# A macaron block of mixture-of-experts, attention and a gated scan: second expert weights kept in SBUF, row tables cleared first, and part of the tails' normalisation moved to ACT

## The chip, the core and the metric

The kernel runs on one core of one Trainium2 chip. The metric is the device time of one execution in microseconds. A core has TensorE (PE, matrix products; its weight loads are listed apart as PEld), VectorE (DVE), ScalarE (ACT), GpSimd (POOL) and SyncE (SP, which here issues nearly all plain DMAs). POOL issues the indirect DMAs, which scatter or gather rows by an index. All data are 32-bit floats; a matrix product of such data runs as two passes, so a count of matmuls in the profile is twice that of the program.

## The reference

The input `x` is 8 sequences of 512 tokens with 128 features. Six residual steps follow each other, each on a layer norm (LN) of `x`:

```
x = x + 0.5 * moe(LN(x))       # 8 experts, 128 -> 512 -> 128, ReLU, each token goes to its best 2
x = x + attention(LN(x))       # 16 heads of 8, rotary positions, causal softmax
x = x + 0.5 * moe(LN(x))       # the same weights
x = x + 0.5 * fp6_linear(LN(x))
x = x + mix(LN(x))
x = x + 0.5 * fp6_linear(LN(x))

moe:        logits = x @ router_w + router_b;  two best, gates = softmax of the two
            y_e = relu(x @ W1[e] + b1[e]) @ W2[e] + b2[e];  out = sum of gate * y_e
fp6_linear: x and weight are rounded, in blocks of 32, to a 6-bit float grid times
            max|block| / 7.5; then x @ weight.T + bias
mix:        n = rmsnorm(x) * w; g, v, d = three linear maps of n
            h_t = a_t * h_(t-1) + sigmoid(g) * tanh(v), a = 0.001 + 0.998 * sigmoid(d)
            u = x + h; m = rmsnorm(u) * w2; out = u + (silu(m @ W_gate) * (m @ W_up)) @ W_out
```

## The kernel before

`X[b]`, the 512 tokens of sequence `b`, stays in SBUF as four tiles of 128 tokens by 128 features. Everything else is written as operations of a graph (`add`): each has one or more engines that it may run on with estimated costs, the buffers that it reads, writes and acquires, and dependencies. `Graph.search` is a list planner. It walks through the graph with a clock of its own, gives each operation an engine and a place, each buffer a slot of its kind, and repeats this 12 times with adapted priorities. The order that it finds best is issued as it is, engine by engine, and semaphores keep the data right; so a change of one cost or one dependency moves many instructions.

Stage 0 is the first expert layer (`moe_front`, `moe_tiles`, `moe_combine` with s = 0), then `attention`, then stage 2, the second expert layer, then a `tail` for each sequence (`fp6` with s = 3, `mix`, `fp6` with s = 5, store). The planner lets stages of different sequences overlap.

The expert layer. Sequences are taken in groups: 2, 3 and 3 of them in stage 0, four groups of 2 in stage 2. `moe_front` normalises, computes logits, picks two experts for each token, and gives each token two places in a table of rows in DRAM in which an expert's rows lie together, padded to tiles of 128. POOL scatters the rows (L783), one indirect DMA for 128 rows. DVE also writes `eids`, the expert of each tile. There are 23 tiles for a group of two and 31 for one of three, 177 in all. `moe_tiles` takes tiles in pairs. For each tile SP reads the expert's number into a register and loads that expert's whole weights into `wx` (L813, L814):

```
r = nc.sync.value_load(state["eids"].t[0:1, i : i + 1], min_val=0, max_val=NE - 1)
nc.sync.dma_start(out=wxi.t, in_=wexp[bass.ds(r, 1), :, :]...)
```

`wx` is 128 x 1156: W1, W2, b2 and b1; six of them exist. SP loads the rows `xs` (L824), PE turns them (`xp`, L835), ACT or DVE copies them to `xt`, PE multiplies by W1 (`hp`, L846), ACT applies bias and ReLU (`hs`, L858), PE multiplies by W2 (`yp`, L867), DVE adds b2 (`yo`, L876), SP stores to a second table (L881). When all tiles of the group are stored, `moe_combine` gathers each token's two rows (POOL, L898) and adds them with their gates (DVE, L911). The table `rows_in` has to be zero where no row is scattered: each of the four tables is cleared by a DMA from a 128 x 128 tile of zeros (L467), the first one behind the loads of `x`, the others later ("late" loads, with the constants of attention and tails).

Attention works in bursts: `sa` (scores for the maxima, L1018), DVE takes row maxima of them (L1070), `sb` (scores again, transposed), ACT's exponential (L1081), POOL cuts the diagonal blocks (L1089), and `av` (L1125). Expert tiles of stage 0 and of stage 2 run between bursts.

The tails. `normed` takes statistics on DVE: four `bn_stats` (L558), four `bn_aggr` (L564), a small sum (L570, or L566 to L568 for a root mean of squares), then POOL raises to the power -1/2 (L581). `scaled_rows` scales the four tiles, on ACT (L598, L600, after L592 on DVE) or on DVE (L602, L604), as the planner chooses. `quantized` finds each block's largest value (L1207), scale and inverse and the negated scale (L1202 to L1204), multiplies by the inverse (L1211, POOL or DVE), finds from the exponent bits how coarse the grid is there (`iz`, and its inverse `iv`, L1224), multiplies (L1226), rounds with a large constant (L1228), corrects ties (L1231, L1233), multiplies by `iv` (L1235, DVE) and then by the negated scale (L1238, POOL or DVE). PE turns the result and multiplies it by the quantized weight (L1271).

Of the kernel before, what the change touches and what calls it, by code (L numbers as in the profile page):

```python
# [39 lines left out]
E_W1, E_W2, E_B2, E_B1 = 0, NFC * P, 2 * NFC * P, 2 * NFC * P + P  # L40
E_ALL = E_B1 + NFC

# [15 lines left out]
TURNED = (0,)  # L58

# [43 lines left out]
class Op:  # L103

    __slots__ = "alts fn acq bufs deps succ left prio start end eng ready bulk order skew idx pace occ".split()
# [26 lines left out]
class Graph:  # L132
# [4 lines left out]
    def add(self, alts, fn, r=(), w=(), acq=(), deps=(), order=(), bulk=0, skew=0.0, pace=0.0):  # L137
# [3 lines left out]
        o.succ, o.start, o.end, o.eng, o.idx = [], None, None, None, len(self.ops)  # L141
        needs = {id(d): d for d in deps}
# [26 lines left out]
    def levels(self):  # L169
        for o in reversed(self.ops):  # L170
            e, t, lat, _ = o.alts[0]
            if e == "PE":
                lat = t + 0.3
            if o.bulk:
                lat = 2.2 + o.bulk / 330e3
            o.prio = max(
                [s.prio + (lat if o in s.deps else 0.0) for s in o.succ], default=lat
            ) + o.skew

# [19 lines left out]
    def refine(self, order, span, first):  # L199
# [13 lines left out]
        for o, f in zip(self.ops, first):  # L213
            o.prio = MIX * (span - late[id(o)]) + (1 - MIX) * o.prio
# [132 lines left out]
def kernel(  # L347
# [3 lines left out]
    wexp: bass.AP,  # L351
    rw: bass.AP,
# [53 lines left out]
    late = []  # L406
# [7 lines left out]
    def load_late(b, ap, bulk):  # L414
        late.append(lambda after: add(
# [6 lines left out]
    def const(name, ap, is_late=False):  # L422
# [4 lines left out]
        return (load_late if is_late else load)(b, ap, n)  # L427
# [23 lines left out]
    zero = filled("zero", [P, P], 0.0)  # L451
# [3 lines left out]
    n_0 = len(GROUPS[0])  # L455
    rows_in, rows_out = [], []
    for g in range(n_g):
        n = max(tiles_of(len(gs[g])) for gs in GROUPS.values() if g < len(gs)) * TW
# [3 lines left out]
    def clear_rows(g, order, skew=0.0):  # L462
        t = rows_in[g].t
        n = t.shape[0]
        return add(
            dma(0),
            lambda e: nc.sync.dma_start(  # L467
                out=t.rearrange("(n p) c -> p n c", p=P),
                in_=zero.t.unsqueeze(1).to_broadcast([P, n // P, P]),
            ),  # L470
            r=[zero], w=[rows_in[g]], bulk=n * P * 4, order=order, skew=skew,
        )

    for b in range(2, nb):
        load_x(b)
    sp.append(clear_rows(0, sp[-1:], 1e4))
    for g in range(1, n_g):
        late.append(lambda after, g=g: clear_rows(g, [groups[0, min(g, n_0) - 1]["sent"][-1]]))
    rope_s = const("rope_s", rope, True)
    wattn_s = const("wattn_s", wattn, True)  # L480
    future_s = const("future_s", future, True)
    vec_s = const("vec_s", vecs, True)
    wq8_s = const("wq8_s", wq8, True)
    wmix_s = const("wmix_s", wmix, True)
    wout_s = const("wout_s", wout, True)
    half_bq = fixed("half_bq", [P, P])
    load_late(half_bq, bq.partition_broadcast(P), P * P * 4)
# [6 lines left out]
    def clear_for_attention(after):  # L494
# [4 lines left out]
        for v in vpad:  # L499
# [5 lines left out]
            for k in range(2):  # L505
# [3 lines left out]
                    w=[v], order=[after])  # L509

# [41 lines left out]
    def normed(src, view, name, eps, skew=0.0, squares=False):  # L552
# [7 lines left out]
        def go(e):  # L560
# [4 lines left out]
            if squares:  # L565
                nc.vector.tensor_tensor(sm.t[:, 36:40], mv[:, :, 0], mv[:, :, 0], ALU.mult)  # L566
                nc.vector.tensor_tensor(sm.t[:, 32:36], sm.t[:, 36:40], mv[:, :, 1], ALU.add)
                nc.vector.tensor_scalar_add(sm.t[:, 32:36], sm.t[:, 32:36], eps)  # L568
            else:
                nc.vector.tensor_scalar_add(sm.t[:, 32:36], mv[:, :, 1], eps)  # L570
# [4 lines left out]
        add(("DVE", 0.4 + 0.2 * squares, 0.5 + 0.2 * squares, None), go, w=[sm], skew=skew)  # L575
# [53 lines left out]
    def moe_front(s, g):  # L629
# [5 lines left out]
        GT, NTL = n_b * NT, tiles_of(n_b)  # L635
# [141 lines left out]
        for n in range(n_b):  # L777
            for k in range(2):
                for t in range(NT):
                    i = n * NT + t  # L780

                    def scatter(e, n=n, k=k, t=t, i=i):
                        ins = nc.gpsimd.indirect_dma_start(  # L783
                            out=rows_in[g].t[0 : NTL * TW, :],
# [7 lines left out]
                        ("POOL", 1.02, 2.2, None), scatter, r=[us[n], (keep, f"at{k}"), (rows_in[g], ("s", name, i, k))],  # L792
# [3 lines left out]
    def moe_tiles(s, g):  # L796

        NTL = tiles_of(len(GROUPS[s][g]))
        state = groups[s, g]
        for j in range((NTL + 1) // 2):  # L800
            tiles = [i for i in (2 * j, 2 * j + 1) if i < NTL]
# [7 lines left out]
            for i in tiles:  # L809
                wx[i] = buf("wx", "wx", f"wx_{name}")  # L810

                def fetch(e, i=i, wxi=wx[i]):
                    r = nc.sync.value_load(state["eids"].t[0:1, i : i + 1], min_val=0, max_val=NE - 1)  # L813
                    nc.sync.dma_start(  # L814
                        out=wxi.t, in_=wexp[bass.ds(r, 1), :, :].rearrange("o p c -> p (o c)")
# [3 lines left out]
                    ("SP", 0.73, 3.0, None), fetch, r=[state["eids"]], w=[wx[i]], acq=[wx[i]],  # L819
# [3 lines left out]
            def rows_of(e, xs=xs, rows=rows, halves=halves):  # L823
                ins = nc.sync.dma_start(  # L824
                    out=halves(xs.t), in_=rows_in[g].t[rows, :].rearrange("(h p) c -> p h c", p=P)
# [4 lines left out]
                dma(0), rows_of, w=[xs], acq=[xs], deps=state["sent"], bulk=w * P * P * 4, order=rows_loads[-1:]  # L830
# [32 lines left out]
            for h, i in enumerate(tiles):  # L863

                def second(e, h=h, i=i, yp=yp, hs=hs, wx=wx):
                    for fc in range(NFC):
                        nc.tensor.matmul(  # L867
                            yp.t[:, ts(h, P)], hs[i].t[:, ts(fc, P)],
                            wx[i].t[:, E_W2 + fc * P : E_W2 + (fc + 1) * P],
# [3 lines left out]
                add(pe(P, NFC), second, r=[hs[i], wx[i]], w=[(yp, h)], acq=[yp, yo] if h == 0 else [])  # L873
# [6 lines left out]
            def store(e, yo=yo, rows=rows, halves=halves):  # L880
                state["stored"].append(nc.sync.dma_start(  # L881
                    out=rows_out[g].t[rows, :].rearrange("(h p) c -> p h c", p=P), in_=halves(yo.t)
# [477 lines left out]
    for g in range(n_0):  # L1360
        moe_front(0, g)
        if g + 1 < n_0:
            late.pop(0)(None)
# [100 lines left out]
```

## Time and profile before

| what | value |
|---|---|
| runs | 1100.86, 1101.2, 1102.36 us (median 1101.2) |
| the profiled execution | 1096.83 us, its span 1095.1 us |
| mean granted TensorE clock | 0.932 |
| busy | PE 929.3, PEld 694.7, DVE 752.4, ACT 515.3, POOL 536.1 us |
| bytes moved by DMA | 163.60 MB |
| of these, weight loads `wx` | 177 of 578 KB each |
| scatters and gathers | 128 and 128 |

The span runs from the first to the last instruction. A page slices it into 40 equal parts and prints for each the busy share in tenths. "issue" in a list of waits is time in which the engine waited for nothing that the profile shows. A queue name such as SPq is the engine's sequencer, which handles registers, semaphores and DMA issues.

### The profile page before, as it was taken

To read this page: it belongs to the slowest core of one execution; us is meant where nothing else is said; L and a number is where in the kernel's file an instruction comes from. 1 tells how busy PE (TensorE), PEld (TensorE's weight loads), DVE (VectorE), ACT (ScalarE), POOL (GpSimd) and SP (SyncE) were. 2 spreads that over 40 slices of the span, in tenths; PEclk is the share of its full clock that TensorE was granted. 3 is DMA by queue.
4 is the path that set the end of the run, shared out by engine and by line. 5 is a ranking of instruction groups with operands and counts; after the bars stand their busy time and mean duration, and the time that the engine had idled before them with its cause. 6 is when DMAs were issued, how large, how long until landed. Compare 5 with 4: busy or idle time off the path is not lost.

```text
span 1095.1 us, 22590 instructions
## 1 busy us (share of the span) xinstructions
PE 929.3 (85%) x7282; PEld 694.7 (63%) x7282; DVE 752.4 (69%) x2797; ACT 515.3 (47%) x1335; POOL 536.1 (49%) x681
## 2 busy tenths in 40 slices
PE   5357958799899989998999999998978989976873
PEld 5357946677667764554765776666877878535452
DVE  7501216278866579997786667966338859999996
ACT  3123523235465654555755665564435536543521
POOL 2771053525722168447246223784048654774552
PEclk9978968799999998999998999999989989988985
DMA  4737969487455411015233354233978876100001
GB/s 147 261 113 250 384 196 331 132 297 225 132 191 158 145 56 50 26 36 182 64 117 100 107 155 141 76 122 93 303 266 270 264 245 214 30 17 1 20 19 39
DMA packets 102070, 163.60 MB, mean 149 GB/s; under 512 B 11200, under 2 KB 70720, under 8 KB 101952
## 3 DMA queue, kind: packets, MB, share of 16 engines
q1 hardware_dynamic: 93760, 145.37, 41.1%
q0 software_dynamic: 8192, 16.79, 5.1%
q8 instruction: 58, 0.95, 0.3%
q14 instruction: 60, 0.49, 0.1%
HBM read 129.28 MB, written 29.16 MB: 145 GB/s over the span
## 4 chain that ended last, share of the span: by engine, by line
PE 50%; DVE 21%; issue 10%; POOL 8%; DMA 6%; another core or an unknown queue 2%; ACT 1%; SPq 1%; POOLq 0%; DVEq 0%; ACTq 0%
PE hp L846 11%; PE yp L867 10%; PE sb L1018 8%; PE sa L1018 7%; PE av L1125 5%; DMA wx<-in_wexp 3%; DVE sa L1070 3%; POOL y L898 3%; POOL rows_in L783 1%; PE xp L835 1%; PE lp L663 1%; DMA y<-rows_out,keep 1%; DVE q L1226 1%; DVE x L911 1%
## 5 line engine op out<-in xcount | busy, mean ns | idle before, releaser
L858 ACT ACTIVATE hs<-hp,wx 128x128 f32<-128x128 f32 x704 | 199.5, 372 | 231.0 <-PE hp L846 115.4
L1070 DVE CUSTOM_DVE_ANT_0 sa<-sa,future_s 128x384 f32<-128x384 f32 (+3 forms) x512 | 241.1, 514 | 86.6 <-PE sa L1018 50.8
L867 PE MATMUL yp<-wx,hs 128*128 128x128 f32 x1416 | 199.1, 287 | 56.3 <-issue 30.2
L1081 ACT ACTIVATE pm<-sb 128x512 f32<-128x512 f32 x320 | 173.3, 598 | 147.5 <-PE sb L1018 67.3
L867 PEld LDWEIGHTS yp<-wx,hs 128*128 128x128 f32 x1416 | 180.7, 200 | 67.8 <-issue 53.6
L846 PE MATMUL hp<-xt,wx 128*128 128x128 f32 x1416 | 200.5, 289 | 9.2 <-DMA wx<-in_wexp 5.1
L1018 PE MATMUL sb<-qa,ka 32*128 32x256 f32 (+3 forms) x1024 | 198.0, 467 | 10.3 <-DVE nstat L1070 6.8
L846 PEld LDWEIGHTS hp<-xt,wx 128*128 128x128 f32 x1416 | 183.1, 202 | 31.4 <-issue 11.8
L1089 POOL TENSOR_SCALAR_AFFINE_SELECT pm<-pm 128x256 f32<-128x256 f32 x256 | 104.3, 426 | 199.2 <-ACT pm L1081 196.6
L1018 PE MATMUL sa<-ka,qm 32*128 32x384 f32 (+3 forms) x1024 | 191.9, 474 | 4.2 <-DVE qm L537 2.4
L898 POOL DMA_INDIRECT y<-rows_out,keep x128 | 136.2, 1064 | 89.7 <-PE yp L867 47.9
L783 POOL DMA_INDIRECT rows_in<-um,keep x128 | 128.7, 1005 | 70.4 <-DVE route L751 32.9
L876 DVE TENSOR_TENSOR yo<-yp,wx 128x128 f32<-128x128 f32 x177 | 48.7, 285 | 124.1 <-PE yp L867 65.3
L1018 PEld LDWEIGHTS sb<-qa,ka 32*128 32x128 f32 x1024 | 98.3, 186 | 49.2 <-DVE nstat L1070 16.7
L1018 PEld LDWEIGHTS sa<-ka,qm 32*128 32x128 f32 x1024 | 88.3, 189 | 31.7 <-issue 7.9
L1125 PE MATMUL av<-pm,vpad 128*32 128x256 f32 (+3 forms) x1024 | 80.4, 445 | 1.8 <-POOL pm L1089 1.3
L535 DVE COPY xt<-xp 128x256 f32<-128x256 f32 (+1 forms) x83 | 33.8, 408 | 59.2 <-PE xp L835 27.4
L1070 DVE DVE_READ_ACCUMULATOR2_ANT nstat<- 128x1 f32 x512 | 72.0, 141 | 0.0
L1125 PEld LDWEIGHTS av<-pm,vpad 128*32 128x32 f32 x1024 | 28.7, 111 | 59.2 <-issue 41.1
L911 DVE SCALAR_TENSOR_TENSOR x<-y,keep,x 128x128 f32<-128x128 f32 x128 | 45.3, 368 | 20.6 <-DMA y<-rows_out,keep 18.6
L835 PE MATMUL xp<-cst,xs 128*128 128x128 f32 x177 | 36.3, 287 | 12.5 <-DMA xs<-rows_in 12.0
L835 PEld LDWEIGHTS xp<-cst,xs 128*128 128x128 f32 x177 | 22.6, 148 | 17.3 <-issue 14.6
(215 smaller groups left out, 1233.6 us busy)
## 6 DMA issues: line engine op xcount, KB each, us to landing
wx<-in_wexp SPq DMA_DIRECT2D x177, 578.0 KB
xs<-rows_in SPq DMA_DIRECT2D x85, 128.0 KB
rows_out<-yo SPq DMA_DIRECT2D x85, 128.0 KB
rows_in<-zero SPq DMA_DIRECT2D x2, 1984.0 KB
rows_in<-zero SPq DMA_DIRECT2D x2, 1472.0 KB
x<-in_x SPq DMA_DIRECT2D x8, 256.0 KB
rows_in<-um,keep POOLq DMA_INDIRECT x128
y<-rows_out,keep POOLq DMA_INDIRECT x128
```

The source lines that it names most:

```text
L783: ins = nc.gpsimd.indirect_dma_start(out=rows_in[g].t[0 : NTL * TW, :], out_offset=bass.IndirectOffsetOnAxis(ap=at(k)[:, i : i + 1], axis= ...
L835: nc.tensor.transpose(xp.t[:, ts(h, P)], halves(xs.t)[:, h, :], ident)
L846: nc.tensor.matmul(hp.t[:, ts(fc, P)], wx[i].t[:, E_W1 + fc * P : E_W1 + (fc + 1) * P], xt.t[:, ts(h, P)], start=True, stop=True,)
L858: nc.scalar.activation(o, a, AF.Relu, bias=bias)
L867: nc.tensor.matmul(yp.t[:, ts(h, P)], hs[i].t[:, ts(fc, P)], wx[i].t[:, E_W2 + fc * P : E_W2 + (fc + 1) * P], start=(fc == 0), stop=(fc == ...
L898: ins = nc.gpsimd.indirect_dma_start(out=tokens(y)[:, t, :], out_offset=None, in_=rows_out[g].t[0 : NTL * TW, :], in_offset=bass.IndirectO ...
L911: nc.vector.scalar_tensor_tensor(X[b].t[:, t, :], tokens(y)[:, t, :], state["gates"](k)[:, i : i + 1], X[b].t[:, t, :], ALU.mult, ALU.add,)
L1018: nc.tensor.matmul(sc.t[:, at : at + hi - lo], stat.t[rows, ts(m, P)], mov.t[rows, lo:hi], start=True, stop=True,)
L1070: nc.vector.tensor_tensor_reduce(out=sc.t[:, at : at + wd], in0=sc.t[:, at : at + wd], in1=future_s.t[:, S - wd : S], scale=-1.0, scalar=3 ...
L1081: nc.scalar.activation(pm.t[:, (h % 2) * S : (h % 2 + 1) * S], sc.t, AF.Exp, scale=scale)
L1089: nc.gpsimd.affine_select(out=diag, in_=diag, pattern=[[0, 2], [1, P]], compare_op=ALU.is_ge, fill=0.0, base=0, channel_multiplier=-1,)
L1125: nc.tensor.matmul(av.t[32 * j : 32 * j + 32, m * P :], v.t[:, row, :], pm.t[:, at : at + S - m * P], start=first, stop=last,)
```

## The change

The second weights of all eight experts are loaded once into `w2_s` (128 x 4096), in two halves, behind the loads of `x`. A tile's `wx` holds only W1, b2 and b1 (128 x 644). The product `yp` takes its W2 from `w2_s` at an address computed from a register; PE loads the expert numbers of up to eight tiles into registers at a time, and so does SP for its own loads. There are three pairs of row tables instead of four: the last group of stage 2 uses those of the first. All are cleared behind the loads of `x`, from a tile of 128 x 1024 zeros in longer runs, and the weights `w2_s` follow. The other constants are loaded in two batches, "attention" and "tail", the latter and the halving of three of them after the first sequence's bursts.

In the tails the statistics of the second root mean (`root_mean`) are sums of squares on ACT. For the last layer norm (s = 5) ACT sums each row for the mean and its squared deviations for the variance (`normed_on_act`), and it scales the rows (`rows_on_act`). In `quantized` the sign of `iv` is turned by its constant, the block's scale is multiplied into `iv` (POOL or DVE), and one product on DVE gives the result. `BOOST` is zero for all sequences and `UPS` is empty, so both do nothing.

```diff
-E_W1, E_W2, E_B2, E_B1 = 0, NFC * P, 2 * NFC * P, 2 * NFC * P + P
+E_W1, E_B2, E_B1 = 0, NFC * P, NFC * P + P
 E_ALL = E_B1 + NFC
+W2 = NFC * P
+REGS = 8
+ON_ACT = (5,)
...
+    table = lambda s, g: g if g < n_0 else 0
...
+    zero = buf("pm", "pm", "zero")
+    add(pool(2 * S, each=1e-3), lambda e: nc.gpsimd.memset(zero.t, 0.0), w=[zero], acq=[zero], skew=9e3)
+    for g in range(n_0):
...
+        sp.append(add(
             dma(0),
-                out=t.rearrange("(n p) c -> p n c", p=P),
-                in_=zero.t.unsqueeze(1).to_broadcast([P, n // P, P]),
+                out=t.rearrange("(p n) c -> p (n c)", p=P).rearrange("p (q c) -> p q c", q=4),
+                in_=zero.t[:, 0 : n // 4].unsqueeze(1).to_broadcast([P, 4, n // 4]),
...
+    w2_s = fixed("w2_s", [P, NE * W2])
+    for q in range(2):
+        half = slice(q * NE * W2 // 2, (q + 1) * NE * W2 // 2)
+        load((w2_s, q), wsec[:, half], P * NE * W2 * 2, to=w2_s.t[:, half])
...
+    def root_mean(src, spare, name, eps, skew=0.0):
+        sm = small(f"sm_{name}")
+        for t in range(NT):
+            add(("ACT", 0.42, 0.55, None), lambda e, t=t: nc.scalar.activation(
+                tokens(spare)[:, t, :], tokens(src)[:, t, :], AF.Square, accum_out=sm.t[:, 32 + t : 33 + t]),
+                r=[(src, t)], w=[(sm, t), (spare, t)], acq=[sm] if t == 0 else [], skew=skew)
+        add(dve(NT), lambda e: nc.vector.tensor_scalar(
+            sm.t[:, 32:36], sm.t[:, 32:36], 1.0 / P, eps, ALU.mult, ALU.add), w=[sm], skew=skew)
+        power(sm, 32, 36, skew)
...
+    def normed_on_act(src, view, spare, name, eps, acq=(), skew=0.0):
...
+            add(("ACT", 0.42, 0.55, None), lambda e, t=t: nc.scalar.activation(
+                tokens(spare)[:, t, :], view()[:, t, :], AF.Copy, scale=-1.0 / P, accum_out=sm.t[:, 24 + 2 * t : 25 + 2 * t]),
...
+            add(("ACT", 0.42, 0.55, None), lambda e, t=t: nc.scalar.activation(
+                tokens(spare)[:, t, :], view()[:, t, :], AF.Square, bias=sm.t[:, 24 + 2 * t : 25 + 2 * t],
+                accum_out=sm.t[:, 32 + t : 33 + t]),
...
+        power(sm, 32, 36, skew)
+        add(dve(NT), lambda e: nc.vector.tensor_tensor(
+            sm.t[:, 60:64], mean(), sm.t[:, 32:36], ALU.mult), w=[sm], skew=skew)
...
     def moe_tiles(s, g):
...
+        def registers(engine, to, at):
+            to.update(zip(at, nc.values_load_multi_w_load_instructions(
+                state["eids"].t[0:1, at[0] : at[-1] + 1], engines=[engine], min_val=0, max_val=NE - 1,
...
+            if (2 * j) % REGS == 0:
+                at = list(range(2 * j, min(2 * j + REGS, NTL)))
+                loads.append(add(
+                    ("SP", 0.6, 0.6, None), lambda e, at=at: registers(mybir.EngineType.SP, expert, at),
...
+                o = add(("PE", 0.3, 0.0, "F"), lambda e, at=at: registers(mybir.EngineType.PE, which, at),
+                        r=[state["eids"]], order=seconds[-4:-3])
...
-                    r = nc.sync.value_load(state["eids"].t[0:1, i : i + 1], min_val=0, max_val=NE - 1)
                     nc.sync.dma_start(
-                        out=wxi.t, in_=wexp[bass.ds(r, 1), :, :].rearrange("o p c -> p (o c)")
+                        out=wxi.t, in_=wexp[bass.ds(expert[i], 1), :, :].rearrange("o p c -> p (o c)")
...
                         nc.tensor.matmul(
                             yp.t[:, ts(h, P)], hs[i].t[:, ts(fc, P)],
-                            wx[i].t[:, E_W2 + fc * P : E_W2 + (fc + 1) * P],
+                            w2_s.t[:, bass.ds(which[i] * W2 + fc * P, P)],
...
             nc.vector.reciprocal(col(2), col(1))
-            nc.vector.tensor_scalar_mul(col(3), col(1), -1.0)
...
-        add(dve(n, two=True), lambda e: v.tensor_scalar(vi(), zi(), -1.0, 0x7F000000, ALU.mult, ALU.add),
+        add(dve(n, two=True), lambda e: v.tensor_scalar(vi(), zi(), -1.0, -0x01000000, ALU.mult, ALU.add),
             r=[iz], w=[iv], skew=skew)
+        add([pool(n, each=1.7e-3), dve(n, own=True)],
+            lambda e: engines[e].tensor_tensor(blocks(iv), blocks(iv), along(col(1)), ALU.mult), r=[sm], w=[iv], skew=skew)
...
-        add(dve(n, own=True), lambda e: v.tensor_tensor(blocks(r), blocks(r), blocks(iv), ALU.mult),
-            r=[iv], w=[r], skew=skew)
-        add([pool(n, each=1.7e-3), dve(n, own=True)],
-            lambda e: engines[e].tensor_tensor(blocks(y), blocks(r), along(col(3)), ALU.mult), r=[r, sm], w=[y], skew=skew)
+        add(dve(n, own=True), lambda e: v.tensor_tensor(blocks(y), blocks(r), blocks(iv), ALU.mult),
+            r=[r, iv], w=[y], skew=skew)
...
-        m2 = normed(u, lambda: tokens(u), f"n{nm}", 1e-6, skew=sk, squares=True)
+        m2 = root_mean(u, xn, f"n{nm}", 1e-6, skew=sk)
```

The new `yp` product stands at L932 of the changed kernel and the register loads at L852.

## The prediction

> **What bounds the kernel now.** I began with the slices of the span, which split the program in three.
>
> ```profile
> PE   5357958799899989998999999998978989976873
> DVE  7501216278866579997786667966338859999996
> DMA  4737969487455411015233354233978876100001
> ```
>
> One digit is 27.4 us. Up to about 220 us PE has holes while DMA is busy by fits. From 220 to 750 PE stays at 8 and 9 (attention with expert tiles between its bursts). From 750 to 925 DMA is high again, and from 925 DVE stands at 9 and PE falls. The table by stretches of 25 us gives sizes; its columns are length, then busy us of PE, weight load, DVE, ACT and POOL, then PE clock, DMA share and GB/s.
>
> ```profile
> 75.00:100.00 25.00, 14.96 (x91) 14.30 (x92) 3.22 (x11) 5.70 (x20) 8.74 (x9) 0.71 0.52 170
> 125.00:150.00 25.00, 16.84 (x136) 16.66 (x136) 3.57 (x11) 7.99 (x28) 12.24 (x13) 0.82 0.89 310
> 350.00:375.00 25.00, 24.94 (x255) 18.22 (x256) 14.93 (x61) 14.56 (x39) 6.05 (x14) 1.00 0.54 161
> 775.00:800.00 25.00, 23.85 (x209) 23.46 (x210) 8.79 (x42) 11.98 (x42) 2.96 (x3) 1.00 0.97 329
> 800.00:825.00 25.00, 18.08 (x141) 17.86 (x140) 11.08 (x47) 9.04 (x30) 13.59 (x14) 0.86 0.75 233
> 1025.00:1050.00 25.00, 21.24 (x103) 14.61 (x103) 24.76 (x63) 10.61 (x24) 13.17 (x12) 0.93 0.06 22
> ```
>
> At 775 the wire is full (0.97); at 1025 DVE is full (24.76 of 25). At 75 and 125 neither is, which the chain of waits has to explain. Its pieces (start, length, what):
>
> ```profile
> 67.59 10.70 issue
> 139.59 13.78 another core or an unknown queue
> ...
> 760.79 0.04 SPq L814
> 760.83 0.06 issue
> ...
> 761.00 5.07 DMA wx<-in_wexp
> 766.12 1.16 PE hp L846 x8
> ...
> 796.67 0.89 PE hp L846 x8
> 797.56 0.89 PE yp L867 x8
> ```
>
> The two long pieces have no named releaser. Both lie where POOL issues indirect DMAs (L783, L898) end to end, one each 1.28 us: in them ACT and DVE stand still too, although the matmuls that they wait for have ended. I call this the POOL stall; its cause the trace does not show. At 761 the releaser is plain: PE waits 5.07 us for expert weights. A tile costs PE 0.89 for hp, 0.89 for yp and 0.22 for its transposition: 2.0 us.
>
> **The change, part by part.** The profiled execution took 1096.8 (span 1095.1 and 1.7 around it), 4.4 under the median 1101.2 of the runs; I take stage savings from the trace off the median.
>
> *Half of the expert weights stay in SBUF.* A pair of tiles now moves two loads of 592 kB (578 KB on the page) and 131 kB each of rows in and out, 1.45 MB; at the 329 GB/s of the 775 row that is 4.4 us against 4.0 of PE. Afterwards it is two loads of 330 kB and the same rows, 0.92 MB, 2.8 us: PE is late next, at 2.0 us a tile. PE stands idle 22.7 us from 750 to 925 (175 less the table's PE column); 6.9 of it is the 800 row, with POOL stall in it. Of the other 16 I take 10, since the waits for tails' DVE work stay; bounds 0 and 16.
>
> *Before attention.* From 55, when the first tile starts, to 250, PE is idle 44 us (the table's PE column again). The planner's order of the changed kernel has 55 tiles ahead of the first score burst instead of 39, and 65 instead of 78 within attention, 57 instead of 60 behind it. Sixteen tiles are 32 us of PE work put in front. If they fill the idle 44, attention and the rest get shorter by 13 + 3 tiles, 32 us. If the holes stay (POOL's scatters and gathers are as many as before, and 17 of the 24 scatters of the third group now come straight behind the second's), the first burst is 32 later and nothing is won. I take the middle, 16; bounds 0 and 32.
>
> *Clearing first.* Three clears (5.6 MB) and the resident weights (2.1 MB) now stand on SP ahead of everything else, 7.7 MB, 24 us at 329 GB/s; SP was idle from 7 to 28 us before, and the first rows are read at 51.7, after 16 scatters by POOL. So the wire has 40 us for them: nothing. What it costs if that cover fails is the first wx loads, issued from 28, landing a few us late, still before 51.7. Tables 0 being used again by the last group adds a wait of its scatters on row loads that ended hundreds of us earlier: nothing.
>
> *Registers on PE.* Each of 708 yp matmuls now has a fused register instruction ahead of it (3 or 4 operations) and an address from a register; 23 register loads stand on PE's queue as well, and 177 leave SP's. SP's rows price such work: two multiplications 0.04 and 0.06 to the next instruction, three comparisons 0.15; so 0.1 to 0.22 per matmul. What hides it is that PE's sequencer runs ahead: in the trace it goes from one semaphore wait at 808.17 to the next, 32 weight loads and matmuls on, in 0.13 us. For a pair of tiles it then needs 8 x 0.1 to 0.22, 0.8 to 1.8 us, of the 4.0 that PE takes. It is bare only after a wait that held the sequencer, when a yp group starts at 4 x 0.22 against 0.89 of matmuls: about the same speed. No row has the decoding of a matmul with a register address; the nearest, SP's DMA with one against one without (0.33 and 0.33 to 0.38), shows no extra. Bounds 0 and 708 x 0.1 = 71; I take 4, near the SP row. A register load holds PE's sequencer until DVE has written the expert numbers, and what queues behind the first is a transposition and the logits of the second group, wanted by DVE. SP's own row (0.28, then 0.2 to 0.4) makes 23 x 0.6 = 14 us, nearly all under bursts; I take 2, bounds 0 and 14.
>
> [...]
>
> *Tails.* The groups that matter (mean ns of one behind the busy us):
>
> ```profile
> L558 DVE BATCH_NORM_STATS2 sm_t<-x 128x6 f32<-128x128 f32 x64 | 16.1, 280 | 0.3
> L564 DVE BATCH_NORM_AGGREGATE sm_t<-sm_t 128x2 f32<-128x6 f32 x64 | 5.8, 152 | 0.0
> L598 ACT ACTIVATE q<-x,sm_t 128x128 f32<-128x128 f32 x28 | 11.5, 482 | 17.2 <-DVE sm_t L592 17.2
> L858 ACT ACTIVATE hs<-hp,wx 128x128 f32<-128x128 f32 x704 | 199.5, 372 | 231.0 <-PE hp L846 115.4
> L1238 POOL TENSOR_TENSOR q<-q,qs 128x512 f32<-128x512 f32 x13 | 13.8, 1062 | 32.0 <-DVE q L1235 30.1 <-DVE sm_t L592 1.9
> ```
>
> By busy time per instruction, DVE loses for the last layer norm 32 x 0.252 + 32 x 0.091 = 11.0 and seven L592 at 0.30, 2.1; for the root mean (L558, L564, L566, L567 on sm_n) 7.5 + 2.9 + 4.6 = 15.0; row scalings 4 x 0.43, 1.7; the negated scale L1204, 1.9; three broadcast products that go to POOL, 3.0. That is 34.7. It gains eight small products (0.16 to 0.42, 2.3) and, by the planner's choice, four row scalings, one copy and six 512-wide additions, 6.2. Net 26 us. From 925 to 1075 DVE is busy 145.7 of 150, so nearly all the part that falls there counts, some 22; PE (112.5 of 150, part of it at a low clock) and ACT's latency are late next. I take 17; bounds 5 and 23.
>
> ACT gains 96 activations with a sum. Between 0.28 (busy of L858 each) and 0.55 (L598's 0.41 plus 0.14, what DVE's accumulator read takes) they are 27 to 53 us; ACT is busy 63.8 of 150 there, so they fit. For the batch that ends last they make a longer row: eight at 0.28 to 0.55 against DVE's 1.8, up to 2.6 more, less L1238's 1.06 that leaves the chain of the quantizer because the scale is multiplied in beside it. About nothing at the end.
>
> [...]
>
> **Sum.** 16 + 10 + 17 - 4 - 2 = 37: 1101.2 - 37 = 1064.
>
> **Rivals.** *Slower:* the sequencer. If a register-addressed matmul shows 0.1 us more than its 0.22 in all places, 71 us go against the 43 won: 1101 - 43 + 71 = 1129. It decides from 43 / 708 = 0.06 us each. For it: no row has such a matmul, and PE is the full engine for 500 us; against it, the run-ahead of 0.13 us for 32. 0.15.
> *The POOL stall holds:* PE's early holes remain or grow, since scatters now follow each other without a gap, and the 10 of the second expert stage shrink to 4: 1101 - 4 - 17 + 6 = 1086. For it: the two chain pieces without releaser, untouched by the change. 0.2.
> *All is hidden:* 1101 - 32 - 16 - 23 = 1030. For it: a wire at 2.8 of 4.0 us. 0.2.
> *My forecast:* 0.45.
>
> **Numbers.** Slower takes 0.15, and out of the stall's 0.2 I give 0.02 to a standstill within 0.2% (2.2 us, about what a measurement here can tell from no change), where gains and register cost cancel; faster 0.83. Low 1030 is the case of all hidden; high 1108 lets in a register cost of some 0.07 us each and leaves the rest of that rival out.
>
> **What would show it.** Right: wx nearly gone from the chain; DMA share at 775 down to 0.6 or so with PE over 24 of 25; first score burst at 180 to 205 us; attention some 25 us shorter; DVE total down by about 26, ACT up by 27 to 53; yp at 0.89 per tile. Wrong: yp tiles at 1.1 us or more with "issue" before L932, PE idle before it (the sequencer); long pieces without releaser of over 40 us in sum ahead of attention (the stall); DVE below 90% in the last 120 us with ACT named before it (ACT became the bound of the tail).

## The result and the profile after

The changed kernel took 1114.9 us (median of 6 runs, 1110.66 to 1119.4); the kernel before, over its 6 runs, 1101.62. The ratio is 1.013, 95% interval 1.0096 to 1.0163: slower, where 1064 and faster were forecast. The profiled execution took 1118.48 (span 1116.8), 21.7 more than before's 1096.83. The medians differ by 13.3 only: the profiled execution of before lies near the fast end of its runs, that of the changed kernel near the slow end, so some 8 us of the differences below are spread between runs.

The slices again (one digit is now 27.9 us):

```profile
PE   6472978988999998999998999999978879699983
...
DVE  7510123267876657896786767994444386999996
...
DMA  9541766751433421002223224230666555100000
```

DMA has become light nearly everywhere, and PE has not become fuller. Four of the stretches that were shown of before, with the same columns:

```profile
75.00:100.00 25.00, 8.53 (x50) 7.34 (x50) 0.47 (x2) 1.14 (x4) 19.04 (x20) 0.66 0.30 96
125.00:150.00 25.00, 23.61 (x203) 22.74 (x203) 5.65 (x18) 12.71 (x48) 2.26 (x3) 1.00 0.85 239
...
775.00:800.00 25.00, 24.88 (x239) 21.83 (x232) 11.01 (x46) 13.89 (x40) 4.08 (x9) 1.00 0.42 111
...
1025.00:1050.00 25.00, 24.37 (x118) 15.25 (x117) 23.93 (x61) 19.24 (x65) 11.69 (x10) 1.00 0.03 11
```

At 775 the wire fell from 0.97 to 0.42, as forecast. At 75 PE worked 8.53 of 25 us at a clock of 0.66, while POOL issued scatters. The chain of waits there, and twice later in the second expert layer:

```profile
75.03 14.73 another core or an unknown queue
...
89.84 20.92 another core or an unknown queue
...
802.23 3.80 DMA wx<-in_wexp
...
918.60 3.92 DMA wx<-in_wexp
```

The long pieces without a releaser grew from 10.70 and 13.78 to 14.73 and 20.92. The first score burst, forecast for 180 to 205 us, came at 235.1; before it came at 185.1. And the weights are not gone from the chain. In the list of what PE waited for (us, times, longest), before and then after:

```profile
PE hp L846 <- DMA wx<-in_wexp: 5.1, 7, 1.5
```

```profile
PE hp L911 <- DMA wx<-in_wexp: 21.7, 19, 5.2
```

Nearly half of the bytes are gone, and PE waits four times as long for the rest. On the chain, loads of `wx` are 8 pieces of 37.0 us in sum before, 4.6 each, and 17 pieces of 62.5 after, 3.7 each: a load has become 0.9 us shorter and is last twice as often.

The best cut is one whose ends are the same events in both kernels: from the first tile to the last tile of stage 0, the stretch without tiles, the tiles of stage 2, and what is left behind the last tile. The first part holds the same work in both (85 tiles, and 344, 240 and 216 passes of `sa`, `sb` and `av`), the second nearly so; the last two share the rest, and how much of the tails' work falls into which differs. Before, then after, in the columns of the stretches:

```profile
55.10:384.10 329.00, 280.70 (x2275) 228.09 (x2276) 159.25 (x607) 145.24 (x433) 126.71 (x170) 0.91 0.65 212
384.10:523.30 139.20, 128.56 (x1073) 72.91 (x1073) 120.34 (x453) 71.38 (x142) 88.88 (x126) 0.96 0.21 70
523.30:931.00 407.70, 376.98 (x3319) 295.03 (x3316) 284.88 (x1102) 224.97 (x602) 199.97 (x267) 0.97 0.54 170
931.00:1095.10 164.10, 115.63 (x510) 75.94 (x510) 152.03 (x429) 62.42 (x135) 90.91 (x78) 0.84 0.06 21
```

```profile
54.60:402.10 347.50, 289.74 (x2293) 233.54 (x2292) 158.99 (x603) 152.97 (x447) 136.08 (x184) 0.90 0.46 129
402.10:547.60 145.50, 133.78 (x1058) 78.24 (x1057) 112.34 (x439) 69.93 (x142) 84.74 (x123) 0.87 0.17 52
547.60:942.30 394.70, 360.18 (x3214) 283.78 (x3211) 257.29 (x999) 211.32 (x581) 190.35 (x258) 0.96 0.42 118
942.30:1116.80 174.50, 136.53 (x616) 89.18 (x614) 154.04 (x379) 104.87 (x344) 99.49 (x83) 0.86 0.06 21
```

The differences are +18.5, +6.3, -13.0 and +10.4 us; with -0.5 ahead of the first tile they make the 21.7. The third part is shorter because tails' work left it: behind the last tile 616 passes of PE are now left instead of 510, in a stretch where DVE is busy for 152 and 154 us of 164 and 175. I call the four parts A, B, C and D.

### The profile page after: what moved, and what is told of

It is laid out like the page before. It is cut to its first block, busy times and chain, and to the rows that moved or that the text cites. A ratio compares the mean times of both kernels' runs of the same rounds, so it can differ in the third digit from the quotient of the medians.

```text
span 1116.8 us, 22851 instructions
## 1 busy us (share of the span) xinstructions
PE 947.0 (85%) x7282; PEld 707.6 (63%) x7282; DVE 718.3 (64%) x2628; ACT 550.4 (49%) x1537; POOL 540.7 (48%) x683
## 4 chain that ended last, share of the span: by engine, by line
PE 53%; DVE 17%; issue 9%; DMA 9%; POOL 4%; another core or an unknown queue 4%; ACT 3%; SPq 1%; POOLq 0%; DVEq 0%; ACTq 0%
PE hp L911 13%; PE yp L932 12%; PE sb L1084 8%; PE sa L1084 6%; DMA wx<-in_wexp 6%; PE av L1191 6%; DVE sa L1136 3%; POOL y L964 2%; PE xp L900 2%; PE lp L711 1%; DMA y<-rows_out,keep 1%; PE pak L1003 1%; ACT pm L1147 1%; DVE mix L1411 1%
## 5 line engine op out<-in xcount | busy, mean ns | idle before, releaser
L923 ACT ACTIVATE hs<-hp,wx 128x128 f32<-128x128 f32 x696 | 196.4, 376 | 219.4 <-PE hp L911 94.2
L911 PE MATMUL hp<-xt,wx 128*128 128x128 f32 x1416 | 210.6, 295 | 53.6 <-issue 26.0
L911 PEld LDWEIGHTS hp<-xt,wx 128*128 128x128 f32 x1416 | 186.6, 205 | 70.0 <-issue 33.6
L932 PE MATMUL yp<-w_s,hs 128*128 x1416 | 197.1, 287 | 18.2 <-issue 13.8
L1084 PE MATMUL sb<-qa,ka 32*128 32x256 f32 (+3 forms) x1024 | 200.3, 478 | 13.3 <-ACT pm L1147 5.1
L1084 PE MATMUL sa<-ka,qm 32*128 32x384 f32 (+3 forms) x1024 | 194.9, 485 | 6.4 <-ACT hs L923 3.2
L932 PEld LDWEIGHTS yp<-w_s,hs 128*128 128x128 f32 x1416 | 181.5, 202 | 28.1 <-issue 21.1
L1084 PEld LDWEIGHTS sb<-qa,ka 32*128 32x128 f32 x1024 | 101.0, 191 | 50.3 <-DVE nstat L1136 15.1
L977 DVE SCALAR_TENSOR_TENSOR x<-y,keep,x 128x128 f32<-128x128 f32 x128 | 48.1, 387 | 23.2 <-DMA y<-rows_out,keep 22.7
L900 PEld LDWEIGHTS xp<-cst,xs 128*128 128x128 f32 x177 | 23.1, 151 | 21.8 <-issue 16.7
```

The lines of the kernel that those rows point to most:

```text
L900: nc.tensor.transpose(xp.t[:, ts(h, P)], halves(xs.t)[:, h, :], ident)
L911: nc.tensor.matmul(hp.t[:, ts(fc, P)], wx[i].t[:, E_W1 + fc * P : E_W1 + (fc + 1) * P], xt.t[:, ts(h, P)], start=True, stop=True,)
L923: nc.scalar.activation(o, a, AF.Relu, bias=bias)
L932: nc.tensor.matmul(yp.t[:, ts(h, P)], hs[i].t[:, ts(fc, P)], w2_s.t[:, bass.ds(which[i] * W2 + fc * P, P)], start=(fc == 0), stop=(fc == N ...
L1084: nc.tensor.matmul(sc.t[:, at : at + hi - lo], stat.t[rows, ts(m, P)], mov.t[rows, lo:hi], start=True, stop=True,)
```

## The experiments

They ran in five groups, each on one chip, with the kernel before measured beside them, so ratios to it are compared, and times only within a group; the first group is also set beside the times of the section above, whose kernel before took the same (1101.62 and 1102.44). The chips were of two sorts. On the chip of the first group the kernel before took 1102 us, as in the given runs; on the four others 1020 to 1022. The visible difference is in the standstills without releaser, shown below.

**First group: undo one part each (before 1102.44).**

Hold the third group's scatters (`held` is the last gather of the first group):

```diff
-                        bulk=P * P * 4,
+                        bulk=P * P * 4, order=held,
...
-    for g in range(n_0):
-        moe_front(0, g)
+    moe_front(0, 0)
+    moe_front(0, 1)
+    moe_tiles(0, 0)
+    moe_combine(0, 0)
+    moe_front(0, 2, [groups[0, 0]["taken"]])
...
```

> The changed kernel with the scatters of the third group held behind the gathers of the first, as they stood before; 55 tiles remain ahead of the first burst, 62 within attention and 60 behind. Theory POOL: 9 scatters instead of 26 follow each other in the stretch after 74 us, so the standstill of 75 to 111 shrinks to 10 or 15 us, the first burst starts 15 to 25 earlier, the run takes 1092 to 1107. Rival (order of tiles): no change of the first burst by more than 5, 1110 to 1120.

Measured 1123.67, ratio 1.0236 (1.0178 to 1.0294). Part A fell to 338.0 from 347.5, but in the profiled execution the other parts gave back 8.9 of the 9.5, and the median is 8.8 above that of the changed kernel. Neither theory had that.

Second weights in `wx` again (and with them the old size of a load, and no register loads on PE):

```diff
...
-                            w2_s.t[:, bass.ds(which[i] * W2 + fc * P, P)],
+                            wx[i].t[:, E_W2 + fc * P : E_W2 + (fc + 1) * P],
```

> The changed kernel with the second weights loaded with each tile again (wx of 592 kB, static addresses of yp, no w2_s, no register loads on PE); tails and clearing as changed. The planner then puts 45 tiles ahead of the first burst, 73 within attention, 59 behind. If the resident weights save wire and what is lost lies elsewhere: 1120 to 1135. If the loss comes with the resident weights (by the order that the planner makes of them): 1090 to 1105, near the kernel before less what the tails bring.

Measured 1104.77, ratio 1.0015 (0.9977 to 1.0052), some 10 us under the changed kernel: most of the loss comes with the resident weights, though they take bytes off the wire. It lies in part D, which is 152.5 instead of 174.5; part C is 410.6 instead of 394.7, with more of PE's work in it (3328 passes instead of 3214). Part A stays at 346.8: that it is 17.8 longer than in the kernel before does not come with the resident weights.

Tails of before:

```diff
-        m2 = root_mean(u, xn, f"n{nm}", 1e-6, skew=sk)
+        m2 = normed(u, lambda: tokens(u), f"n{nm}", 1e-6, skew=sk, squares=True)
```

(This is one line of the edit; `quantized` and the last layer norm likewise.)

> The changed kernel with the tails of before (statistics of the root mean and of the last layer norm on DVE, the negated scale, the product by the scale behind the chain). If the tails bring the 17 us of the forecast: 1125 to 1140, DVE busy some 26 to 34 more. If DVE's saved time is not on the path that ends last: within 5 of 1115. If the longer chains on ACT cost: 1100 to 1110.

Measured 1137.67, ratio 1.0348 (1.0295 to 1.0402): 22.8 more than the changed kernel. Part D grew to 194.4, DVE busy 177.60 of it. The tails bring what was forecast for them, and more, in this order of the program.

**Second group: do one part alone (before 1021.91).**

> The kernel before with the changed tails alone (second weights loaded with each tile, four tables, late clears); 39 tiles ahead of the first burst, 79 within attention, 59 behind. Undoing the tails cost the changed kernel 20 to 25 us; if that is a saving of the tails themselves, this run takes 1075 to 1085 and the stretch behind the last score burst is some 20 shorter than 347. Rival (the tails help only where the planner has put them late, as the changed kernel does): 1095 to 1103.

Edit: `root_mean`, `normed_on_act`, `rows_on_act` and the new `quantized` in the kernel before. Measured 1016.67, ratio 0.9950 (0.9930 to 0.9971): 5.2 us, not 20. The second theory has the right direction; its times were for the other sort of chip.

> The kernel before with the second weights resident alone (registers on PE, w2_s loaded behind x; tails, tables and late clears as before); 54 tiles ahead of the first burst, 66 within attention, 57 behind. Theory (resident weights lose by the order that the planner makes of them: more tiles ahead of the first burst, tails pushed behind the tiles): 1120 to 1140, first burst at 220 to 235. Rival (the weights save wire, and the loss lies in the cleared tables): 1080 to 1100.

Edit: `w2_s`, `registers` and the narrow `wx` in the kernel before. Measured 1059.05, ratio 1.0339 (1.0297 to 1.0381). Resident weights alone, in the order that the planner makes of them, lose 37 us. Part D is 196.8, with 632 passes of PE in it.

Pauses on POOL in the changed kernel (`pause` is a tile of 128x256; the same stands behind each gather):

```diff
                         state["scattered"].append(unordered(ins, f"out{name}"))
+                        nc.gpsimd.memset(pause.t, 0.0)
+                        nc.gpsimd.memset(pause.t, 0.0)
```

> The changed kernel with two cleared tiles of 128x256 (about 0.6 us together) on POOL behind each scatter and each gather, in the order of the changed kernel; nothing else differs. Theory POOL (in the stretch from 75 to 111 us, where POOL issues scatters end to end every 1.28 us, PE, ACT, DVE and SP get an instruction only every 0.7 us or so; with pauses they don't): the first score burst starts 15 to 25 us earlier than 235, PE is busy over 18 of 25 from 75 to 100 instead of 8.5, and the run takes 1090 to 1105. Rival (55 expert tiles in PE's order ahead of the first burst set its start, and POOL's issues only lie beside them): the first burst 0 to 15 later, 1115 to 1130.

Measured 1162.92, ratio 1.1362 (1.1322 to 1.1403). On this chip there was nothing for a pause to cure, so the run could not test the theory, and no pause was timed on a chip with standstills; it shows what POOL's time is worth. In the chain's shares POOL stands at 32%, against 8% in the changed kernel on such a chip (third group):

```profile
POOL 32%; PE 32%; DVE 14%; DMA 10%; issue 9%; ACT 2%; SPq 1%; POOLq 0%; DVEq 0%; ACTq 0%
```

Fixed addresses for `yp`:

```diff
-                            w2_s.t[:, bass.ds(which[i] * W2 + fc * P, P)],
+                            w2_s.t[:, (i % NE) * W2 + fc * P : (i % NE) * W2 + (fc + 1) * P],
```

> The changed kernel in the same order with the second product at fixed addresses of w2_s (tile i takes expert i mod 8, so the values are those of other experts): the register loads on PE stay, the 708 fused register instructions and the register addresses go. Theory (PE's sequencer runs ahead, registers cost next to nothing): within 4 of 1115. Rival (a register-addressed matmul costs 0.06 us or more): 1075 or less.

Measured 1024.9, ratio 1.0021 (1.0003 to 1.0039). On this chip neither bound can be read as a time; the ratio is to be set beside 1.0083 and 1.0100 of the changed kernel below, on two other chips, a difference of 6 to 8 us.

**Third group: the planner's order (before 1020.66).**

> The changed kernel itself, beside the others and on their chip, as their reference. Chips differ: on one the kernel before took 1102 us, on another 1022, with no standstills. If the chip is of the second sort: ratio to before 0.998 to 1.008 (the same order with fixed addresses gave 1.002 there), which prices the registers at under 4 us. If it is of the first: 1.010 to 1.016.

Measured 1030.27, ratio 1.0083 (1.0057 to 1.0109). So the change loses about 1% on a chip without standstills too. The stretch in which PE worked 8.53 us reads here:

```profile
75.00:100.00 25.00, 22.89 (x196) 22.07 (x195) 5.20 (x16) 13.17 (x47) 19.18 (x20) 1.00 0.90 262
```

POOL issues the same 20 scatters in it, end to end, and PE, ACT and DVE go on beside them. What I called the POOL stall needs the chip as well as the scatters; on this chip it is not what the change loses by. Parts A and D of this run:

```profile
54.40:344.50 290.10, 271.21 (x2292) 217.48 (x2292) 159.53 (x603) 152.93 (x447) 136.52 (x184) 0.98 0.54 155
...
855.20:1030.00 174.80, 134.56 (x616) 88.27 (x614) 155.05 (x379) 105.03 (x344) 100.55 (x83) 0.87 0.06 21
```

The old estimate for a load in the planner, and nothing else:

```diff
-                    bulk=P * E_ALL * 4, order=loads[-1:],
+                    bulk=P * (E_ALL + W2) * 4, order=loads[-1:],
```

> The changed kernel, but the planner's estimate for a load of wx stays that of 592 kB although 330 kB are moved; so only the order changes: 45 tiles ahead of the first burst, 71 within attention, 61 behind, and 177 instead of 219 of the tails' quantizer and mix operations on DVE behind the last expert tile. Theory (the order that the planner makes of cheap weights is what loses: tails pushed behind the tiles, into a stretch where DVE is full): ratio to the changed kernel 0.975 to 0.99, that is 0.975 to 0.995 of before. Rival (registers on PE or the resident weights themselves cost): ratio to the changed kernel 0.995 to 1.005.

Measured 1017.84, ratio 0.9962 (0.9934 to 0.9990): 12.4 us less than the changed kernel, by order alone, and on the same chip. PE waited 0.9 us for weights, once, and in part D 538 passes of PE are left. Part D is where the time went:

```profile
855.90:1014.40 158.50, 113.90 (x538) 77.15 (x538) 137.77 (x322) 91.23 (x307) 93.24 (x78) 0.88 0.07 22
```

Of the 15.6 us between the two profiled executions, D makes 16.3 (174.8 to 158.5), A 3.9 and B 1.3, and C gives 5.4 back.

> The kernel before with changed tails and resident weights, late clears and four tables as before, and the planner's estimate for wx left at 592 kB: 41 tiles ahead of the first burst, 82 within attention, 54 behind, 188 tail operations on DVE behind the last tile. With the tails alone before gave 0.995. Theory (order): 0.975 to 0.99, a few us of wire better than tails alone. Rival (the wire was hidden in the first place): 0.99 to 1.0. If resident weights cost by themselves: above 1.005.

Measured 1005.9, ratio 0.9829 (0.9774 to 0.9884). With the order of the old estimate, resident weights are worth 1.2% on top of the tails by these ratios (0.9950 for the tails alone, on another chip); the same program gave 0.9878 on a third chip (fourth group), which makes it 0.7%. On the chip of this group the same estimate with early clears and three tables took 11.9 us more (1017.84).

> The changed kernel with 60 us of priority for each tail instead of 0 (the planner's BOOST, 60 eight times): 55 tiles ahead of the first burst, 64, 58; only 98 instead of 219 tail operations on DVE are left behind the last tile, 171 instead of 62 stand between the last burst and the last tile. Theory (tails pushed to the end): the stretch behind the last tile falls from 171 to some 90 us, that before it grows by less; ratio to the changed kernel 0.98 to 0.99. Rival (sum of PE and DVE work behind the last burst is what counts, wherever it stands): 0.995 to 1.01.

Edit: `BOOST = [60, 60, 60, 60, 60, 60, 60, 60]`. Measured 1059.78, ratio 1.0357 (1.0303 to 1.0411). Parts C and D:

```profile
484.30:932.30 448.00, 421.40 (x3574) 323.87 (x3571) 348.39 (x1225) 272.25 (x770) 233.84 (x290) 0.99 0.37 106
932.30:1059.30 127.00, 60.65 (x257) 40.08 (x254) 79.23 (x197) 36.79 (x117) 51.48 (x46) 0.70 0.07 23
```

My theory that tails ought only to come earlier fell. Behind the last tile DVE is busy 79.23 of 127 and PE 60.65 of 127, so neither is full there: I read it as too few sequences left to overlap (the chain of one sequence was not measured alone). C and D together are 575 us, against 546 in the changed kernel on this chip.

**Fourth group: what is left (before 1020.41).**

> The changed kernel with the old estimate for wx in the planner and the third group's scatters held behind the first group's gathers: 43 tiles ahead of the first burst, 73 within attention, 61 behind; 9 scatters instead of 33 stand between the first 30 and the gathers. Theory (scatters ahead of gathers on POOL make the first stage longer): the stretch from the first to the last tile of stage 0 falls from 286 to 275 us or less, ratio to before 0.98 to 0.99. Rival (early clearing and the batches of constants cost by themselves): the stretch stays at 283 or more, ratio 0.993 to 1.0.

Edit: the held scatters and the old estimate together. Measured 996.8, ratio 0.9764 (0.9719 to 0.9810). Parts A and D:

```profile
54.70:321.30 266.60, 261.35 (x2276) 213.02 (x2276) 159.54 (x605) 145.32 (x434) 130.88 (x177) 0.98 0.57 166
...
837.70:995.80 158.10, 117.56 (x538) 78.97 (x538) 138.54 (x326) 90.27 (x305) 92.48 (x77) 0.85 0.07 22
```

Part A fell from 286.2 (the old estimate alone, on the chip of the third group) to 266.6; PE is idle in it for 5.2 us, against 20.6 there and 18.9 in the changed kernel (290.10 less 271.21). POOL's gathers of the first group ended at 128.2 instead of 137.4, and the first score burst came at 149.3 instead of 163.8. In the list of PE's waits:

```profile
PE hp L911 <- DMA wx<-in_wexp: 2.0, 2, 1.5
```

> The kernel before with changed tails and resident weights, late clears and four tables, and the planner's estimate at the real 330 kB: 54 tiles ahead of the first burst, 66 within attention, 57 behind, 220 tail operations on DVE behind the last tile; some 46 scatters ahead of the first gathers. Theory (order): 1.005 to 1.015 of before, as the changed kernel. Rival (early clearing is what loses): 0.98 to 0.99.

Measured 1038.97, ratio 1.0186 (1.0141 to 1.0232). Late clears with the cheap estimate lose just as well: with that estimate clearing first is not what costs.

> The kernel before with changed tails and resident weights and the planner's old estimate (0.983 of before on another chip), again, as reference for the next run: 0.977 to 0.989 of before.

> The run before this one, in the same order, with the second product at fixed addresses (tile i takes expert i mod 8, so the values are those of other experts). If registers on PE cost what the run-ahead of its sequencer suggests: 0 to 3 us less than that run. If the 5 us between the changed kernel and its fixed-address form on two chips are their price: 4 to 8 us less.

Measured 1007.45 and 1004.08 (ratios 0.9878, 0.9830 to 0.9926, and 0.9847, 0.9802 to 0.9892). The register addresses cost 3.4 us, or 0.005 us for each of 708 matmuls, between the two ranges; the intervals overlap, so it is "a few us" and no more exact. The first of the two differs from the run with late clears and the cheap estimate (1038.97, same chip) by the planner's estimate alone: 31.5 us, of which part A makes 22.3 in the profiled executions (293.7 and 271.4) and part D 18.0 (177.1 and 159.1), and B and C give 8.4 back.

**Fifth group: the same chip for all (before 1021.79).**

> The version with the old estimate for wx and the held scatters (0.976 of before on another chip), beside the changed kernel. On a chip without standstills 0.972 to 0.981 of before; on one with them 0.97 to 1.0, still below the changed kernel by 2% or more.

Measured 994.8, ratio 0.9739 (0.9695 to 0.9783): 27 us faster than before and 36 faster than the changed kernel beside it. It beats both.

> The changed kernel again as reference on this chip: 1.006 to 1.011 of before on a chip without standstills, 1.010 to 1.016 on one with them.

Measured 1030.84, ratio 1.0100 (1.0068 to 1.0133).

> The changed kernel with the third group's scatters held, the planner's estimate as changed (55 tiles ahead of the first burst, 216 tail operations behind the last tile). Theory (the hold shortens the first stage by 10 us or more wherever the tails stand; on the other chip standstills ate it): 0.99 to 1.0 of before. Rival (the first stage's gain is given back behind the last tile, where DVE is full): its first stage is 10 shorter than the changed kernel's and its ratio still 1.003 or more.

Measured 1044.95, ratio 1.0240 (1.0185 to 1.0296). The hold alone does not shorten part A at all (290.1 against 287.3 of the changed kernel beside it). The first theory fell, and the rival too in its first half.

Together, on chips without standstills (ratios to before, from different chips of that sort):

| | scatters free | scatters held |
|---|---|---|
| real estimate, 55 tiles ahead of the first burst | 1.008 and 1.010 | 1.024 |
| old estimate, 45 and 43 tiles ahead | 0.996 | 0.976 and 0.974 |

The old estimate was not run on a chip with standstills, so that the order is what loses there too rests on the run with the second weights in `wx`. And only these two estimates were tried.

## Why the prediction was wrong, step by step

*Before attention, 16 won.* This step failed first. I counted 44 us of PE's holes as room that sixteen tiles could fill, and split the difference. But they were no room. On a chip without standstills the kernel before with the new tails has 11 us of idle PE in the whole of part A (274.2 less 263.2), with the same 39 tiles ahead of the first burst:

```profile
54.70:328.90 274.20, 263.19 (x2277) 214.11 (x2276) 160.75 (x608) 145.66 (x433) 126.98 (x167) 0.99 0.76 255
```

The 44 us were mostly standstills, and sixteen more tiles in front did not fill them: PE's idle time in part A went from 48.3 to 57.8 us. The case that I had set as the lower bound came, the first burst 32 us later and nothing won: without standstills it comes at 147.8 us with 39 tiles ahead (the run with the new tails alone) and at 181.9 with 55 (the changed kernel), 34 later. And the first burst's start is the wrong measure: part A does the same work in either order, and its length went from 329.0 to 347.5.

*Half of the weights, 10 won.* The wire went as said (0.97 to 0.42 at 775, 163.6 to 117.8 MB). The step failed in taking a load's size at 329 GB/s as its price: 330 kB make 1.0 us, but on the chain a load lasted 3.7 us in the mean, and 4.6 when it was 592 kB. Six buffers are taken round, and the next load of a buffer waits for the last reader, `yo` (SP waited 326 us in all for it). The planner made the same error: by its formula a load is there 2.6 us after its issue began (0.52 + 0.8 + 330/330 + 0.3), where it reckoned 3.4 before. With 3.4 as the estimate, PE's wait for weights went from 21.7 us (15.7 on a chip without standstills) to 0.9 and 2.0, and resident weights became worth 7 to 12 us, near the 10 of the forecast. But the waits were not the loss itself: without them parts A and C took 663.0 us together instead of 661.5, and the gain was in part D. That 3.4 helped because it is nearer to what a load takes is not shown; it may be luck of the order. And fewer tails behind the last tile do not help by themselves, as the run with priority for them shows (1.0357).

*Tails, 17 won.* The direction was right: DVE lost 34.1 us in the whole kernel (752.4 to 718.3; 26 forecast), ACT gained 35.1 (27 to 53 forecast), and the tails undone cost 22.8. But I added this to the other terms as if it stood alone. In the order of the kernel before the tails bring 5.2; in the changed order they bring more, 19.9 of it in part D (194.4 to 174.5), where that order leaves more of the tails. That order was the other missing term: I had its tile counts (55, 65, 57) and priced them only by PE's time, at nothing for the tails' work that is left behind the last tile. There 616 passes of PE are left instead of 510, DVE is busy for 154.0 us instead of 152.0 although each tail needs less of it, and the part became 10.4 us longer where I had it some 17 shorter. By the two pairs that differ in the planner's estimate alone this order costs 12.4 and 31.5 us.

With DVE busy for 177.60 of 194.4 us in part D when the tails are undone, the new tails win 22.8 us, though not all of that is by ACT: the shorter quantizer is in it, and the two were not run apart. The new sums on ACT, two groups of the activations and the accumulator reads of one:

```profile
L587 ACT ACTIVATE q<-x,sm_t 128x128 f32<-128x128 f32 x32 | 12.4, 393 | 0.0
...
L583 ACT ACTIVATE q<-x 128x128 f32<-128x128 f32 x32 | 9.4, 302 | 3.8 <-DVE x L1424 3.8
...
L583 ACT ACTIVATION_READ_ACCUMULATOR q<-x 128x1 f32 x32 | 6.2, 194 | 0.0
```

By all six such groups (9.5, 6.0, 9.4, 6.2, 12.4 and 6.2) the 96 activations with their reads cost 49.7 us of ACT, at the upper end of the 27 to 53.

*Registers on PE, 4 lost; register loads, 2.* 3.4 measured for the addresses on one chip, and 6 to 8 by ratios from different chips; the run-ahead argument held, and the rival of the sequencer, at 43 us or more, is out. `yp` shows the same 287 ns a pass in both pages (1416 passes for 708 matmuls). The loads stayed in all runs with registers and were not priced alone.

*Clearing first, nothing.* Right for the wire (the late-clear version with the cheap estimate is at 1.0186). But I charged nothing for 17 scatters of the third group that now stand ahead of the first group's gathers on POOL, the queue that I had named. With the old estimate that is 2% (0.996 to 0.976), and on one chip the kernel with late clears was 11.9 us faster than the one with early clears (1005.9 and 1017.84). With the cheap one it is nothing, or less than nothing, and the traces show why. With the old estimate POOL issues scatters up to 116.4 us and the first gather at once behind them, at 116.7; held, they let it start at 107.6. With the cheap one POOL is through with them at 106.7 and stands idle for 3.3 us until PE's tiles are done; the first gather starts at 110.0, and with the scatters held at 111.6. On the chip of the first profile part A is 17.8 us longer than before even with the second weights in `wx`; early clearing and its scatters are the likeliest cause there, but they were not run apart from the rest.

*The rivals.* "The POOL stall holds" was right that it stays and grows (24.5 to 35.7 us in the two long pieces), and wrong that it decides: without any standstill the change is slower by 0.8 and 1.0% all the same, against 1.3% with them. "All is hidden" (1030) missed that the order itself changes. No rival said that a cheaper load would make the planner's order worse, which is what the runs show on the chips without standstills.

## What to carry to other kernels

Where a planner or scheduler orders the work, a cheaper operation changes the order of everything, so price the new order, and try the new operation under the old estimate: here that one number separated a loss of 0.8% from a gain of 0.4%. Price a load that is waited for by its time on the chain of waits (3.7 us here), not by its bytes (1.0 us). Cut the span into parts with the same work before calling an idle stretch room, and let savings on an engine count only where the remaining order keeps that engine full.

## What was not expected of the hardware

The same program, the kernel before, takes 7% less on some chips (1020 to 1022 us instead of 1102). On the chip of the first profile, PE, ACT, DVE and SP get an instruction only now and then while POOL issues scatters 1.28 us apart: in the 25 us from 75 PE has 50 matmuls, DVE 2 instructions and ACT 4, against 196, 16 and 47 on the chip of the third group, and SP issues two DMAs; between 94 and 111 us PE's weight loads and matmuls start 0.70, 1.40 or 2.10 us after each other, in multiples of 0.70, and the chain names no releaser. On three other chips the same 28 scatters in a row leave PE 21.8 to 22.9 us of work in the 25 us from 75, and "another core or an unknown queue" does not appear in the chain's shares, where it has 4% on the first. The standstills move with the indirect DMAs: with the scatters held, on the chip of the first group, PE works 18.04 of the 25 us from 75, and 10.74 of the 25 us from 175, where the held scatters now stand; two pieces without releaser, of 8.36 and 8.44 us, lie at 176.8 and 185.3. Part A was 9.5 us shorter and still had 46.6 us of idle PE (338.0 less 291.36). Why the standstills lie beside indirect DMAs, and on that chip alone, no run here shows.
